# Seven block products in place of eight for q, k and v of a transformer block

## The chip, the cores and the metric

The kernel runs on one core of a Trainium2 chip. The metric is device time in microseconds for one execution; three runs took 2912.02, 2907.1 and 2908.67 us, so the median is 2908.67 us.

Five engines matter. TensorE (PE in the profile, with its weight loads as PEld) multiplies matrices into PSUM banks. VectorE (DVE) and ScalarE (ACT) read PSUM and write SBUF. GpSimd (POOL) works on SBUF. SyncE (SP) issues nearly all transfers. Each engine takes its instructions in order and waits on semaphores for the others.

## The reference

The input is 16 sequences of 224 tokens with 512 features, a condition vector per sequence, and a context of 750 tokens per sequence. All is float32. The part that changes is the first one, self-attention with 16 heads of 32 features:

```
shift_a, scale_a, gate_a, ... = split(silu(c) @ W_mod + b_mod, 6)
x_norm = layernorm(x) * (1 + scale_a) + shift_a
q, k, v = split(x_norm @ W_qkv + b_qkv, 3)
attn   = softmax(q k^T / sqrt(32)) v
x      = x + gate_a * (attn @ W_proj + b_proj)
```

Behind it come cross-attention to the context and an MLP (512 to 2048 to 512, GELU), each with its norm and residual.

## The kernel before

**Stages.** The kernel has three stages: self-attention (0 to about 728 us), cross-attention and the MLP. The output of each goes through DRAM (`x_self`, `x_cross`) to the next. Only self-attention is touched here.

**Order.** All engines' instructions are kept in the order in which the program gives them (class `Ordered`, lines 19 to 34): whatever is written earlier for an engine runs earlier on it. So the order of the Python calls is the order of each queue. A wrapper records every operation, and therefore nearly all of them carry line 28 in the profile; they are told apart by the names of their tiles.

**Self-attention.** The 16 sequences are taken two at a time (`PB` = 2), as 8 pairs. Two sequences together are 448 columns (`PN`). For a pair, `norm_begin`, `Norm.stats` and `Norm.apply` make the layer norm (statistics on VectorE, the rest on GpSimd, from tile `x` to tile `xn`); `turn_x` transposes a quarter of the features of both sequences on TensorE, and `modulate` writes the four results as four tiles `xt` of 128 x 448. `project_qk(p, m)` (line 445) makes one 128-row block of q or k for both sequences: four matmuls of 128x128 weights on 448 columns into one bank, and one eviction (q on VectorE, times the softmax scale; k on ScalarE). `project_v(p, c)` (line 462) makes v for one chunk of 112 tokens: four matmuls on 512 columns. A pair needs eight of the first and four of the second.

A pair's attention runs in 8 units, four groups `g` of four heads times two sequences `j` (the loop at line 627). A unit issues, in this order:

- `self_scores`: scores of the unit into `sc` (four PSUM banks, one buffer); VectorE reduces them to row maxima and splits these into three bf16 parts `nm`
- `finish`: VectorE normalizes the output of an earlier unit (a reciprocal and a product)
- slot 0 of the plan
- `self_weights` of the unit before: the scores again, transposed, less the maxima, into `sc`, and Exp on ScalarE into `pt`
- `max_rows`: the maxima transposed on TensorE into an "mm" bank, copied by VectorE
- `add_keys`: VectorE adds the two halves of `pt` into `acc`
- slot 1 of the plan
- `self_values`: values and the sums of the weights (from `acc`) into bank `o`

```
            if was:
                pt = self_weights(*was, row)
            row = max_rows(sa, ps_mm, nm)
            if was:
                acc = add_keys(pt)
            run(plan, (p, u, 1))
            if was:
                finish = self_values(*was, pt, acc)
```

**The plan** (`at_slot`, from line 503) fills the slots with work of other kinds: the rest of this pair's q and k, the output projection of the pair before (`project`, which also adds the residual to `x` and stores it), and the norm, transposes, v and first q and k of the next pair. Per pair, units 0, 2 and 4 hold two q or k products, unit 4 also the transposes, units 1 and 3 the output projection, units 5 and 6 v, unit 7 the next pair's first q and k. In the last pair the remaining parts are spread in halves, three to a unit. In the first pair, products for the modulation (`part`) take the place of the output projection.

**Buffers.** PSUM has eight banks: four for `sc`, three that go round under the name `mm` (projections, transposes, maxima), one for `o`. A bank is taken by the next tile once the last reader of its old tile is done. Input tiles `x` have six buffers and stay in SBUF until the residual is added.

The MLP stage already multiplies by seven block products (`combine`, `combine_right`, class `First`).

Of the kernel before, what the change touches and what calls it, by code (L numbers as in the profile page):

```python
# [8 lines left out]
F32 = mybir.dt.float32  # L9
# [28 lines left out]
def kernel(  # L38
# [187 lines left out]

    self_pools = ExitStack()
# [17 lines left out]
    for b in range(PB):  # L245
        xs[b] = load_x(sa, tokens(x, b), 6)
# [63 lines left out]
    def transpose_pair(pool, psum, xn, p, i_shift, i_scale, k):  # L310

        ps = psum.tile([P, 512], F32, name="mm")
        for t in range(PT):
            turn(ps[:, t * TP : (t + 1) * TP], xn[t // TC][:, t % TC, k * P : (k + 1) * P], ident[:TP, :TP])
        xt = pool.tile([P, PN], F32, name="xt", bufs=2 * KC)
        for j in range(PB):
            modulate(ps[:, j * N : (j + 1) * N], xt[:, j * N : (j + 1) * N], PB * p + j, k, i_shift, i_scale)
        return xt

# [10 lines left out]
    def weights_t(pool, psum, row, q_ap, k_ap, chunks, rows, bufs):  # L333

        st = psum.tile([P, HG, 512], F32, name="sc")
        n = len(chunks)
        for s in range(HG):
            mm(
                st[:rows, s, : n * N].rearrange("p (k t) -> p k t", k=n),
                ones16[s * HD : s * HD + NT, :rows],  # L340
                row[s * HD : s * HD + NT, :].unsqueeze(1).to_broadcast([NT, n, N]),
                start=True, stop=False,
            )
        for j, kc in enumerate(chunks):
            for s in range(HG):
                mm(
                    st[:rows, s, j * N : (j + 1) * N], k_ap(s, kc), q_ap(s),
                    start=False, stop=(j == n - 1),
                )
        pt = pool.tile([rows, HG, n * N], F32, name="pt", bufs=bufs)  # L350
        nc.scalar.activation(pt, st[:rows, :, : n * N], AF.Exp)
        return pt
# [83 lines left out]
    if True:  # L436
# [8 lines left out]
        def project_qk(p, m):  # L445
            ps = ps_mm.tile([P, 512], F32, name="mm")
            for k in range(KC):
                mm(
                    ps[:, :PN], (wq, wk)[m // KC][:, k, (m % KC) * P : (m % KC + 1) * P], xts[p][k],
                    start=(k == 0), stop=(k == KC - 1),  # L450
                )
                if k == 1:
                    yield
            t = sa.tile([P, PN], F32, name="qk", bufs=6)
            bm = bcol[:, o_qkv + m : o_qkv + m + 1]
            if m < KC:
                nc.vector.tensor_scalar(t, ps[:, :PN], bm, SCALE, ALU.add, ALU.mult)
            else:
                nc.scalar.activation(t, ps[:, :PN], AF.Identity, bias=bm)
            qk[p, m] = t  # L460

        def project_v(p, c):
            ps = ps_mm.tile([P, 512], F32, name="mm")
            for k in range(KC):
                mm(
                    ps[:TP, :H], xts[p][k][:, c * TP : (c + 1) * TP], wv[:, k, :],
                    start=(k == 0), stop=(k == KC - 1),
                )
            t = sa.tile([TP, H], F32, name="v", bufs=2 * PT)
            nc.scalar.copy(t, ps[:TP, :H])  # L470
            vs[p, c] = t

        def fetch(p):
            for b in range(PB * p, PB * (p + 1)):
                xs[b] = load_x(sa, tokens(x, b), 6)

        def norm_begin(p):
            for b in range(PB * p, PB * (p + 1)):
                xns[b] = sa.tile([TP, TC, H], F32, name="xn", bufs=PB)
                norms[b] = Norm(  # L480
                    [xns[b][:, c, :] for c in range(TC)], [xs[b][:, c, :] for c in range(TC)], TP
                )

        def turn_x(p, k):
            xts.setdefault(p, []).append(
                transpose_pair(
                    sa, ps_mm, [xns[PB * p + j] for j in range(PB)], p, i_shift_a, i_scale_a, k
                )
            )

        def project(p, t):
            b, c = PB * p + t // TC, t % TC
            if c == 0:
                gate[b] = gate_rows(sa, 0, b * N, TP, 2)
            ps = ps_mm.tile([P, 512], F32, name="mm")
            yield from project_heads(ps, at[p], wproj, t * TP)
            add_to_x(sa, ps[:TP, :H], xs[b][:, c, :], bproj, gate[b])
            if c == TC - 1:
                nc.sync.dma_start(out=x_self[b], in_=xs[b])
# [6 lines left out]

        for p in range(NP):
            if p < NP - 1:
                for g in range(1, KC):
                    at_slot(p, 2 * g - 2, 0, lambda p=p, g=g: whole(project_qk(p, g)))  # L510
                    at_slot(p, 2 * g - 2, 1, lambda p=p, g=g: whole(project_qk(p, KC + g)))
                for t in range(PT if p else 0):
                    at_slot(p, 1 + t // 2 * 2, t % 2, lambda p=p, t=t: whole(project(p - 1, t)))
            else:

                left = [(project_qk, p, m) for m in (1, KC + 1, 2, KC + 2)]
                left += [(project, p - 1, t) for t in range(2)]
                left += [(project_qk, p, m) for m in (3, KC + 3)]
                left += [(project, p - 1, t) for t in range(2, PT)]
                parts = [h for f, *args in left for h in halves(lambda f=f, args=args: f(*args))]  # L520
                for i, h in enumerate(parts):
                    at_slot(p, i // 3, i % 3 // 2, h)
# [18 lines left out]
            if n < NP:  # L541
                if n > 1:
                    at_slot(p, 0, 0, lambda n=n: fetch(n))
                at_slot(p, 1, 0, lambda n=n: norm_begin(n))
                for t in range(PT):
                    at_slot(
                        p, 1 + t // 2, t % 2, lambda n=n, t=t: norms[PB * n + t // TC].stats(t % TC)
                    )
                for j in range(PB):
                    at_slot(p, 1 + j, 1, lambda n=n, j=j: norms[PB * n + j].apply())  # L550
                for k in range(KC):
                    at_slot(p, 4, k // 2, lambda n=n, k=k: turn_x(n, k))
                for t in range(PT):
                    at_slot(p, 5 + t // 2, t % 2, lambda n=n, t=t: project_v(n, t))
                at_slot(p, 7, 0, lambda n=n: whole(project_qk(n, 0)))
                at_slot(p, 7, 1, lambda n=n: whole(project_qk(n, KC)))
# [35 lines left out]
        def self_values(p, g, j, pt, acc):  # L592
# [6 lines left out]
            if g == 0 and j == 0:  # L599
                at[p] = []  # L600
            if j == 0:
                at[p].append(sa.tile([P, PN], F32, name="at", bufs=2 * KC))
            return lambda: normalize(sa, o, at[p][g][:, j * N : (j + 1) * N])

        norm_begin(0)
# [8 lines left out]
        fetch(1)  # L614
# [3 lines left out]
        whole(project_qk(0, 0))  # L618
        whole(project_qk(0, KC))
        for t in range(PT):  # L620
            project_v(0, t)
        bproj = value_bias(sa, ps_mm, wproj, b_proj, o_qkv + 2 * KC, "bproj")

        units = [(p, g, j) for p in range(NP) for g in range(KC) for j in range(PB)]
        was = None
        finish = None
        for i, (p, g, j) in enumerate(units):
            u = g * PB + j
# [7 lines left out]
            row = max_rows(sa, ps_mm, nm)  # L636
            if was:
                acc = add_keys(pt)
            run(plan, (p, u, 1))
# [4 lines left out]
            left = len(units) - i  # L644
            if left == 16:
# [5 lines left out]
            if left in (10, 8):  # L651
                cnorms[0, left == 8].all()
            if left in (7, 6):
                Norm([first[7 - left][:TP]], [first[7 - left][:TP]], TP).all()
# [3 lines left out]
        for t in range(PT):  # L658
            whole(project(NP - 1, t))
        assert not plan  # L660
# [28 lines left out]

    def every(steps):  # L690
        for _ in steps:
            pass

    def combine(engine, a11, a12, a21, a22, s1, s2, s3, s4):

        yield engine.tensor_tensor(s1, a21, a22, ALU.add)
        yield engine.tensor_tensor(s3, a11, a21, ALU.subtract)
        yield engine.tensor_tensor(s2, s1, a11, ALU.subtract)
        yield engine.tensor_tensor(s4, a12, s2, ALU.subtract)

    def combine_right(engine, b11, b12, b21, b22, t1, t2, t3, t4):

        yield engine.tensor_tensor(t1, b12, b11, ALU.subtract)
        yield engine.tensor_tensor(t3, b22, b12, ALU.subtract)
        yield engine.tensor_tensor(t2, b22, t1, ALU.subtract)
        yield engine.tensor_tensor(t4, b21, t2, ALU.subtract)
# [636 lines left out]
```

## Time and profile before

| | us |
|---|---|
| median of three runs | 2908.67 (2907.1 to 2912.02) |
| span of the profiled execution, first to last instruction | 2906.1 |
| start, up to the first scores | 43.47 |
| first pair (83.55), then six pairs of 84.54 each | to 634.25 |
| last pair, up to the scores of its last unit | 63.07 |
| from there to the first work of cross-attention | 30.66 |

No time is listed for the profiled execution apart from its span; the span is 1.0 us below the fastest run and 2.6 us below the median.

Over the whole span the busy shares are PE 98%, PEld 62%, DVE 66%, POOL 41%, ACT 39%. A busy PE in these numbers holds matmuls whose ends are modelled, so the starts of the next instructions say more than the lengths. In a timeline line the first number is the start in us from the span's start, the second the length of the group, then engine, line, operation, output and input tiles, shapes, and the count; brackets give the idle time before it and what ended it.

### The profile page before, as it was taken

To read this page: it belongs to the slowest core of one execution; us is meant where nothing else is said; L and a number is where in the kernel's file an instruction comes from. 1 tells how busy PE (TensorE), PEld (TensorE's weight loads), DVE (VectorE), ACT (ScalarE), POOL (GpSimd) and SP (SyncE) were. 2 spreads that over 40 slices of the span, in tenths; PEclk is the share of its full clock that TensorE was granted. 3 is DMA by queue.
4 is the path that set the end of the run, shared out by engine and by line. 5 is a ranking of instruction groups with operands and counts; after the bars stand their busy time and mean duration, and the time that the engine had idled before them with its cause. 6 is when DMAs were issued, how large, how long until landed. Compare 5 with 4: busy or idle time off the path is not lost. (4 is left out here: it accounts for less than half of the span.)

```text
span 2906.1 us, 47040 instructions
## 1 busy us (share of the span) xinstructions
PE 2834.6 (98%) x19733; PEld 1810.3 (62%) x19733; DVE 1926.2 (66%) x2764; ACT 1119.7 (39%) x1402; POOL 1201.5 (41%) x1357
## 2 busy tenths in 40 slices
PE   8999999998999999999999999999979999999999
PEld 3444444444555565555656556556546888888888
DVE  4666776676478778787787787877775643444343
ACT  1222222221356655665566556655643112112211
POOL 1022222122356666676666766666551210221021
PEclk9999999998999999999999999999999999999999
DMA  5111110100100010100101100000013111110110
GB/s 191 59 33 33 32 33 10 60 11 24 57 32 24 23 35 24 35 26 21 35 24 35 35 19 28 27 33 24 22 44 107 55 37 37 44 58 29 45 44 30
DMA packets 55384, 114.43 MB, mean 39 GB/s; under 512 B 4308, under 2 KB 4372, under 8 KB 55172
## 3 DMA queue, kind: packets, MB, share of 16 engines
q1 hardware_dynamic: 54560, 110.58, 11.8%
q8 instruction: 155, 2.54, 0.4%
q10 hardware_dynamic: 612, 0.85, 0.1%
q14 instruction: 57, 0.47, 0.1%
HBM read 89.33 MB, written 22.09 MB: 38 GB/s over the span
## 5 line engine op out<-in xcount | busy, mean ns | idle before, releaser
L28 POOL TENSOR_TENSOR acc<-acc,pt 125x448 f32<-125x448 f32 x504 | 573.6, 1138 | 39.5
L28 ACT COPY pt<-sc 125x1792 f32<-125x1792 f32 x192 | 317.3, 1653 | 563.1 <-DVE top L28 510.1
L28 DVE TENSOR_TENSOR pt<-pt,o 125x896 f32<-125x896 f32 x384 | 394.2, 1081 | 88.1 <-PE o L28 85.5
L28 DVE TENSOR_TENSOR top<-top,sc 125x896 f32<-125x896 f32 x320 | 346.4, 1083 | 35.4 <-PE sc L28 28.7
L28 PE MATMUL mm<-wkvc,cxt 128*125 128x512 f32 x768 | 354.4, 604 | 6.9 <-ACT kt L28 6.9
L28 PE MATMUL mm<-cxt,wkvc 128*128 128x375 f32 x1024 | 355.0, 489 | 2.3 <-ACT cxt L28 2.3
L28 ACT ACTIVATE pt<-pt 125x896 f32<-125x896 f32 x384 | 338.4, 951 | 20.0 <-DVE pt L28 19.4
L28 POOL TENSOR_TENSOR upd<-upd,gate 112x512 f32<-112x512 f32 (+1 forms) x60 | 79.2, 1321 | 632.9 <-DVE upd L28 628.4
L28 POOL TENSOR_TENSOR acc<-pt 125x448 f32<-125x448 f32 x126 | 143.8, 1141 | 447.7 <-ACT pt L28 447.7
L28 PEld LDWEIGHTS mm<-cxt,wkvc 128*128 128x128 f32 x1024 | 185.6, 191 | 119.8 <-issue 16.6
L28 DVE RECIPROCAL at<-o 128x224 f32<-128x224 f32 x128 | 198.6, 1552 | 72.9 <-PE o L28 72.9
L28 PEld LDWEIGHTS mm<-wkvc,cxt 128*125 128x125 f32 x768 | 136.5, 187 | 171.5 <-issue 153.2
L28 ACT ACTIVATE pt<-sc 112x1792 f32<-112x1792 f32 x64 | 106.5, 1663 | 333.8 <-PE sc L28 333.8
L28 POOL TENSOR_TENSOR rstd<-mv,eps 112x2 f32<-112x2 f32 (+3 forms) x93 | 18.0, 193 | 508.8 <-DVE mv L28 508.8
L28 PE MATMUL sc<-qt,kt 32*125 32x224 f32 x3072 | 201.6, 377 | 14.0 <-ACT pt L28 13.4
L28 PE MATMUL mm<-xt,wqkv 128*128 128x448 f32 x512 | 208.6, 550 | 5.7 <-DVE xt L28 4.7
L28 DVE TENSOR_REDUCE m<-sc 112x8 f32<-112x1792 f32 x64 | 129.6, 2025 | 121.8 <-PE sc L28 121.8
L28 PEld LDWEIGHTS sc<-qt,kt 32*125 32x125 f32 x3072 | 133.1, 183 | 94.1 <-issue 33.8
L28 PE MATMUL o<-pt,vt 125*32 125x224 f32 x3072 | 158.6, 354 | 0.0
L28 PEld LDWEIGHTS mm<-xt,wqkv 128*128 128x128 f32 x512 | 92.0, 190 | 87.6 <-issue 80.4
L28 DVE TENSOR_REDUCE mc<-mm 112x8 f32<-112x512 f32 (+1 forms) x128 | 79.8, 665 | 98.3 <-PE mm L28 98.3
L28 ACT COPY mx<-a 128x512 f32<-128x512 f32 x26 | 15.2, 586 | 327.0 <-POOL upd L28 307.9
(185 smaller groups left out, 4656.5 us busy)
## 6 DMA issues: line engine op xcount, KB each, us to landing
cx<-in_ctx_dram SPq DMA_DIRECT2D x96, 250.0 KB
x<-in_x_dram SPq DMA_DIRECT2D x16, 448.0 KB
x_self<-x SPq DMA_DIRECT2D x16, 448.0 KB
x<-x_self SPq DMA_DIRECT2D x16, 448.0 KB
x_cross<-x SPq DMA_DIRECT2D x16, 448.0 KB
mx<-x_cross SPq DMA_DIRECT2D x28, 256.0 KB
w<-in_L_xcond_W_mlp_dram SPq DMA_DIRECT2D x7, 1024.0 KB
xr<-x_cross SPq DMA_DIRECT2D x28, 256.0 KB
```

Of the source, the lines that this page charges most:

```text
L28: return lambda *args, **kw: self.tc.keep_in_program_order(f(*args, **kw))
```

## The change

**Seven products.** For a pair, x is seen as a matrix of two by two blocks: features 0 to 255 and 256 to 511, first and second sequence. Each of the three weight matrices is cut into two by two blocks of 256. With four sums of blocks of x (`data_blocks`) and four of each weight (`weight_blocks`), the four blocks of the result come from seven block products instead of eight (`seven`). `project_qk(p, i, r)` makes rows `r` and `r + 2` of q (`i` = 0) or k (`i` = 1) for both sequences: seven products of two matmuls on 224 columns. `project_v(p, c)` makes two token chunks of v, one of each sequence: seven products of two matmuls on 256 columns.

Products are numbered by the block pair that they multiply, and run in the order 1, 2, 6, 5, 7, 3, 4. Three banks are used: a holds 1, then 6, 7 and 4 on top; c holds 2; b holds 5, then 3 on top. After a product, ScalarE or VectorE copies the bank to its place in the result (`keep`), or VectorE adds the bank to what is there (`add`).

**The plan.** A third slot comes behind `add_keys`, and `add_keys` itself now stands behind slot 1. A seven is cut in four steps: products 1 and 2, and product 6, in slot 0; 5 and 7 in slot 1; 3 and 4 in slot 2. Units 0 and 1 hold rows 1 and 3 of q and of k, units 2 and 3 the output projection and the transposes of the next pair, units 4 and 5 v, units 6 and 7 rows 0 and 2 of the next pair's q and k. Groups of heads go in the order 0, 2, 1, 3. In the last pair the sevens take units 0 to 3 in halves and the output projection of the pair before units 4 to 7.

**Sums.** The block sums of x (four of 128 x 448) are made on GpSimd in unit 3; those of the weights (twelve of 128 x 512) on VectorE before the first unit.

**Norm and residual.** x is loaded straight into `xn` (two buffers), and the norm is made in place. For the residual, `fetch_rest` loads x again, one chunk of 112 tokens at a time into three buffers, a unit ahead of the output projection, and each chunk is stored on its own. The softmax scale moves from the eviction of q into the Exp.

The core of the diff:

```diff
+    def seven(product, bank, keep, add):
+        a = bank()
+        product(a, 1, True)
+        keep((0, 0), a)
+        c = bank()
+        product(c, 2, True)
+        add((0, 0), c)
+        yield
+        product(a, 6, False)
+        keep((0, 1), a)
+        yield
+        b = bank()
+        product(b, 5, True)
+        keep((1, 1), b)
+        product(a, 7, False)
+        add((1, 1), a)
+        yield
+        product(b, 3, False)
+        add((0, 1), b)
+        product(a, 4, False)
+        keep((1, 0), a)
...
+    def data_blocks(engine, tt, x0, x1):
+        every(combine_right(
+            engine, x0[:, lo2], x1[:, lo2], x0[:, hi2], x1[:, hi2],
+            tt[:, 0], tt[:, 1], x1[:, lo2], tt[:, 2],
+        ))
+        return {
+            1: x0[:, lo2], 2: x0[:, hi2], 3: x1[:, hi2], 4: tt[:, 2],
+            5: tt[:, 0], 6: tt[:, 1], 7: x1[:, lo2],
+        }
...
+        def project_qk(p, i, r):
...
+            def keep(at, ps):
+                m = o_qkv + i * KC + r + 2 * at[0]
+                if at == (1, 1):
+                    nc.vector.tensor_scalar(place(at), ps[:, :N], bcol[:, m : m + 1], None, ALU.add)
+                else:
+                    nc.scalar.activation(place(at), ps[:, :N], AF.Identity, bias=bcol[:, m : m + 1])
+            def add(at, ps):
+                nc.vector.tensor_tensor(place(at), ps[:, :N], place(at), ALU.add)
...
+        def fetch_rest(p, t):
+            b, c = PB * p + t // TC, t % TC
+            xr[b, c] = sa.tile([TP, H], F32, name="xr", bufs=3)
+            nc.sync.dma_start(out=xr[b, c], in_=tokens(x, b)[:, c, :])
...
+        def one(u):
+            return (u, 0), (u, 0), (u, 1), (u, 2)
+
         for p in range(NP):
             if p < NP - 1:
-                for g in range(1, KC):
-                    at_slot(p, 2 * g - 2, 0, lambda p=p, g=g: whole(project_qk(p, g)))
-                    at_slot(p, 2 * g - 2, 1, lambda p=p, g=g: whole(project_qk(p, KC + g)))
+                for i in range(2):
+                    steps(p, one(i), lambda p=p, i=i: project_qk(p, i, 1))
                 for t in range(PT if p else 0):
-                    at_slot(p, 1 + t // 2 * 2, t % 2, lambda p=p, t=t: whole(project(p - 1, t)))
+                    at_slot(p, 1 + t // 2, t % 2, lambda p=p, t=t: fetch_rest(p - 1, t))
+                    at_slot(p, 2 + t // 2, t % 2, lambda p=p, t=t: whole(project(p - 1, t)))
...
                 for k in range(KC):
-                    at_slot(p, 4, k // 2, lambda n=n, k=k: turn_x(n, k))
-                for t in range(PT):
-                    at_slot(p, 5 + t // 2, t % 2, lambda n=n, t=t: project_v(n, t))
-                at_slot(p, 7, 0, lambda n=n: whole(project_qk(n, 0)))
-                at_slot(p, 7, 1, lambda n=n: whole(project_qk(n, KC)))
+                    at_slot(p, 2 + k // 2, 1, lambda n=n, k=k: turn_x(n, k))
+                at_slot(p, 3, 1, lambda n=n: x_sums(nc.gpsimd, n))
+                if n + 1 < NP:
+                    at_slot(p, 4, 0, lambda n=n: fetch(n + 1))
+                for c in range(TC):
+                    steps(p, one(4 + c), lambda n=n, c=c: project_v(n, c))
+                for i in range(2):
+                    steps(p, one(6 + i), lambda n=n, i=i: project_qk(n, i, 0))
...
             row = max_rows(sa, ps_mm, nm)
+            run(plan, (p, u, 1))
             if was:
                 acc = add_keys(pt)
-            run(plan, (p, u, 1))
+            run(plan, (p, u, 2))
             if was:
                 finish = self_values(*was, pt, acc)
```

## The prediction

> **What bounds the kernel now.** I read the windows first (which engine fills which stretch), then the engines' timelines of the fourth pair of sequences, and last the places where TensorE waited.
>
> One pair in the steady state, by the windows (columns: length; busy us and instructions of PE, PEld, DVE, ACT, POOL; clock, DMA share, GB/s):
>
> ```profile
> 127.02:211.56 84.54, 83.45 (x645) 41.47 (x641) 59.18 (x96) 18.18 (x16) 17.44 (x20) 1.00 0.10 28
> ...
> 697.00:698.00 1.00, 1.00 (x16) 0.66 (x12) 0.00 (x0) 0.00 (x0) 0.89 (x1) 0.76 0.00 0
> 698.00:699.00 1.00, 1.00 (x12) 0.58 (x7) 0.00 (x0) 0.00 (x0) 0.00 (x0) 0.50 0.35 102
> ```
>
> PE works 83.45 of 84.54 us: each us of its work counts, and each us in which it waits counts as much. DVE is at 70%. One unit of that stage on PE, by the timeline (start, length):
>
> ```profile
> 316.51 1.03 PE L28 MATMUL sc<-qk 32*112 32x224 f32 x16
> 317.47 3.27 PE L28 MATMUL mm<-xt,wqkv 128*128 128x448 f32 x8
> 320.67 0.40 PE L28 MATMUL sc<-mrow,ones 3*112 3x448 bf16 x4
> 320.91 0.93 PE L28 MATMUL sc<-qk 32*112 32x224 f32 x16
> 321.77 0.27 PE L28 MATMUL mm<-ident,nm 112*128 112x112 bf16 x2
> 321.88 3.23 PE L28 MATMUL mm<-xt,wqkv 128*128 128x448 f32 x8
> 325.04 0.96 PE L28 MATMUL o<-pt,v 112*32 112x224 f32 x16
> 325.82 0.56 PE L28 MATMUL o<-acc,ones 112*32 112x224 f32 x8
> ...
> 764.48 1.68 PE L28 MATMUL mm<-xt,wqc 128*128 128x224 f32 x8
> 765.99 1.45 PE L28 MATMUL mm<-ident,cx 125*128 125x125 f32 x12
> ```
>
> No gap, and the next unit's scores start at 326.31: scores 0.96, a block of projections in slot 0, weights 1.10, maxima 0.11, a block in slot 1, values 0.78, sums 0.49. VectorE in the same unit, and in the one unit type where PE does wait:
>
> ```profile
> 317.61 2.02 DVE L28 TENSOR_REDUCE m<-sc 112x8 f32<-112x1792 f32 x1 [0.68 <-PE sc L28]
> ...
> 320.42 1.54 DVE L28 RECIPROCAL at<-o 128x224 f32<-128x224 f32 x1
> 321.99 0.39 DVE L28 TENSOR_TENSOR at<-o,at 128x224 f32<-128x224 f32 x1
> 322.30 0.67 DVE L28 TENSOR_SCALAR qk<-mm,bcol 128x448 f32<-128x448 f32 x1
> ...
> 323.87 1.08 DVE L28 TENSOR_TENSOR acc<-pt 112x896 f32<-112x896 f32 x1
> ...
> 343.44 0.26 PE L28 MATMUL mm<-ident,nm 112*128 112x112 bf16 x2 [0.42 <-DVE qk L28]
> 344.37 3.25 PE L28 MATMUL mm<-xt,wqkv 128*128 128x448 f32 x8 [0.67 <-DVE xt L28]
> ```
>
> See that an eviction of slot 0 stands behind reduction, split and reciprocal: PE left the scores at 317.47 and had done the q product by 320.67, but DVE took it at 322.30, 4.83 after the scores. Today that rarely hurts, as the three "mm" banks go round; in unit 4, where two transposed banks are added, PE waited on just that eviction (0.42) and on the transposes' (0.67).
>
> **The change, part by part.** All times "at" are from the moment PE leaves a unit's scores.
>
> *PE work.* A float matmul is two passes here. Per pair, q and k have 64 passes of 448 columns, 0.376 apart (a block of 8 takes 3.16 to 3.20: 8 x 0.376 = 3.01, and 0.15 to 0.19 at the change from small to full tiles). They become 4 x 7 x 2 x 2 = 112 passes of 224. The row at 764.48 is this shape: 8 in 1.51, 0.189 each. So 24.1 becomes 21.2. v has 32 passes of 512 columns at 0.429 (350.54 to 354.16 for 8) and gets 56 of 256; the MLP's passes of that shape start 1.73 per 8, 0.216 each: 13.7 becomes 12.1. Saved 4.5 a pair, 36 in eight.
>
> *Wait 1: the bank of the fifth product.* A "seven" takes three banks (a, c, b) while the maxima's transposes take one too, and there are three. Slot 0 uses a and c, the maxima the third, so slot 1's b gets c's bank, free once DVE has added c. That add stands behind the reciprocal: it starts at 4.83 and takes 0.39, so P5 starts at 5.25. PE gets there: q or k unit 12 passes (2.46) + 1.10 + 0.11 = 3.67, waits 1.58; v unit 2.78 + 1.21 = 3.99, waits 1.3. Then 16 passes (3.17, or 3.6 for v) with the evictions of P5 and P7 in time (DVE 6.2 to 6.6 and 6.9 to 7.3; P3 and P4 want them at 6.8 and 7.5), values, sums and scores 2.23: 10.63 for q/k units, 11.1 for v units. In units 0 and 1 two bn_stats pairs (0.82 each) also precede the key sums, which end at 9.2 instead of 8.3; PE wants them at 9.2: 10.7. Queued behind PE's wait are P7, P3, P4, values and the next scores, so the whole unit moves.
>
> *Wait 2: the key sums.* add_keys moves behind slot 1 on DVE. In units 2 and 3 slot 1 now holds an output projection and two transposes. PE: 3.61 + 1.10 + 0.11 + 3.57 + 0.86 = 9.25, values until 10.03. DVE must first do upd (8.57), then four xt modulations (1.67, the row at 343.31; until 10.85), then the sums (11.93). PE waits 1.98: 13.46 instead of 11.48.
>
> A pair: 2 x 10.7 + 2 x 13.46 + 2 x 11.1 + 2 x 10.63 = 91.8, of which 12.9 is waiting; before 84.54 (9.80, 10.62, 9.80, 10.62, 12.66, 10.62, 10.62, 9.80). +7.2 each in pairs 1 to 6: **+43**.
>
> *Start.* PE has 22.7 of products (two sevens of q and k, two of v) instead of 19.8 before the first unit. DVE makes 12 weight sums (the MLP's 128x512 rows: 0.68) and POOL four sums of xt (1.14, by acc<-acc,pt 125x448), and P6 wants the third of each: xt is ready at 21.7, POOL's third at 24.1, so q ends at 28.0; wk's third sum at 29.6, k ends at 33.4; wv's at 35.2, v ends at 45.6 instead of 39.9. **+5.7** (ends: 2.9 if all sums hide, 15.7 if all 12.8 us of them show).
>
> *First pair.* No output projection fills units 2 and 3: DVE's chain sets 10.0 and 14.1; unit 1 holds a seven and two modulation parts, 16.2; with 7.4, 2 x 11.1 and 2 x 10.63 it is 91.2 against 83.55: **+7.7**.
>
> *Last pair.* Only two sevens are left, in halves: units of 8.0 and 9.1 in turn, then 8.72 with half projections; in each, reduction to key sums to next scores sets it. Seven units 60.4 instead of 63.07. The last unit keeps filler, so its tail is 13.2 instead of 16.45 (697.32 to 713.77, at half clock): **-5.9**.
>
> *Clock.* The windows show clock 0.76, then 0.50, after PE waits of 1.59 and 0.45 (694 to 697). A wait of 1.62 at 736.10 was followed by none. 1.98 lies between. A fall lasts 3.4 us at least (796.5 to 799.9), 1.7 us of work. Twelve such waits in pairs 1 to 6: 0 to 20; I take half, **+10**. [...]
>
> *Costed at nothing.* Scale inside Exp: the same 1.66 us instruction. Norm in place: the same instructions; x is fetched from unit 4 on, 42 us ahead of its statistics. Residual chunks: 0.9 MB more per pair at 28 GB/s; on SP, chunk 3's load stands behind the store of chunk 1, which waits for POOL, and it is needed a unit (13 us) later; were it late, POOL's sums of xt would follow it and P6 of unit 4 with them. ACT: 18 short copies instead of 8 long, +3 us on 18. DVE: 18 adds of 0.39 to 0.42 and six copies of 0.43 less four evictions of 0.68, +7 on 59, harmless but for its place. POOL's sums of xt stand behind two residual adds and end their third at 2.4 of unit 4, where P6 is wanted at 1.9: the wait for P5 covers that.
>
> Sum: 43 + 5.7 + 7.7 - 5.9 + 10 = +61. The profiled span is 2906.1; the median run is 2.6 longer, and that I add: **2969**.
>
> **The rivals.**
> - *The waits are hidden* (other side): DVE comes to c's add before PE wants b. It decides below 4.4 us of waiting a pair (7.5 of start and ends + 6 x (w - 5.7) = 0) against my 12.9. With none: 6 x -5.7 + 5.7 - 4 - 5.9 = -38, 2870. For it: DVE has 30% free. Against: its order shows in every unit, and three banks are three.
> - *Only wait 1 is missing* (b gets a free bank): w = 4.0, no gain, 2906. *Only wait 2 is missing*: 2935.
> - *The 1.58 waits lower the clock too*: 24 more chances, 1.7 each, all taken: +41, 3010. They are shorter than the 1.62 that did nothing, but by a hair.
> - *Short passes don't pay*: weight loads take 0.19 for 128 columns; at 0.216 per pass +3.0 a pair, 2993. The row at 764.48 says 0.189.
>
> **How the numbers follow.** Mine 0.64 (own range 2945 to 2995); waits hidden 0.06; wait 1 missing 0.05; wait 2 missing 0.08; clock 0.13; slow passes 0.04. Range 2930 to 3015 takes in all but the first two rivals and some overshoot. Faster by over 0.2% (a run tells no less): 0.08; within: 0.03; slower: 0.89.
>
> **What would show it.** Right: pairs of about 92 us; PE idle of 1.3 to 1.6 ahead of each fifth product, released by DVE; in units 2 and 3 some 2 us ahead of o<-acc, released by DVE acc; products 0.19 and 0.216 per pass; DVE's xt modulations ahead of acc; clock falls after units 2 and 3; first scores near 49. Wrong: PE over 97% busy within a pair, or its waits on ACT, POOL or DMA.

## The result, and the profile after

The changed kernel takes 3022.38 us (median of four runs, 3021.26 to 3022.95); the kernel before, on the same chip, 2910.35 us (2907.1 to 2913.03). The ratio is 1.0387, with a 95% interval of 1.0372 to 1.0401: 112 us slower. The forecast was 2969, within 2930 to 3015: the direction was right, and the loss was almost twice the one foretold.

The page's line of busy times and the window of the fourth pair (columns as in the prediction; the same pair took 84.53 before, with PE busy for 83.44 of it):

```profile
PE 2854.6 (94%) x20309; PEld 1930.1 (64%) x20309; DVE 1992.3 (66%) x2936; ACT 1141.1 (38%) x1482; POOL 1247.6 (41%) x1389
...
343.39:442.34 98.95, 86.62 (x717) 56.46 (x713) 66.19 (x116) 20.91 (x26) 22.79 (x24) 0.93 0.12 33
```

The pair has 12.3 us in which PE waits, where there was 1.1. And although less arithmetic is asked of PE, its busy time has gone up by 3.2: the clock in this window is 0.93, where it was 1.00.

**A q or k unit.** PE's timeline in unit 6 of that pair:

```profile
421.76 1.78 PE L28 MATMUL mm<-xt,wqkv 128*128 128x224 f32 x8
423.38 0.97 PE L28 MATMUL mm<-xtt,wb 128*128 128x224 f32 x4
424.28 0.40 PE L28 MATMUL sc<-mrow,ones 3*112 3x448 bf16 x4
424.51 0.93 PE L28 MATMUL sc<-qk 32*112 32x224 f32 x16
425.37 0.27 PE L28 MATMUL mm<-ident,nm 112*128 112x112 bf16 x2
427.02 1.02 PE L28 MATMUL mm<-xtt,wb 128*128 128x224 f32 x4 [1.38 <-DVE qk L28]
427.88 0.92 PE L28 MATMUL mm<-xt,wqkv 128*128 128x224 f32 x4
428.64 0.97 PE L28 MATMUL mm<-xt,wb 128*128 128x224 f32 x4
429.45 0.92 PE L28 MATMUL mm<-xtt,wqkv 128*128 128x224 f32 x4
430.30 0.96 PE L28 MATMUL o<-pt,v 112*32 112x224 f32 x16
```

and VectorE's over the same stretch:

```profile
421.90 2.03 DVE L28 TENSOR_REDUCE m<-sc 112x8 f32<-112x1792 f32 x1 [2.23 <-PE sc L28]
...
424.70 1.55 DVE L28 RECIPROCAL at<-o 128x224 f32<-128x224 f32 x1
426.28 0.39 DVE L28 TENSOR_TENSOR at<-o,at 128x224 f32<-128x224 f32 x1
426.59 0.38 DVE L28 TENSOR_TENSOR qk<-mm,qk 128x224 f32<-128x224 f32 x1
```

The fifth product starts 5.26 after PE left the scores. It waits for the addition of c's bank at 426.59, and that addition was ready to run at about 423.5, when the second product was done, but stood in VectorE's queue behind the reduction, the split and the reciprocal.

**Unit 2** of the next pair. PE at its end and at the start of unit 3, then VectorE and GpSimd at the same time:

```profile
474.03 0.96 PE L28 MATMUL o<-pt,v 112*32 112x224 f32 x16
477.82 0.97 PE L28 MATMUL o<-acc,ones 112*32 112x224 f32 x8 [2.83 <-DVE acc L28]
478.73 1.85 PE L28 MATMUL sc<-qk 32*112 32x224 f32 x16
480.51 5.64 PE L28 MATMUL mm<-wproj,at 128*112 128x512 f32 x8
```

```profile
474.05 1.76 DVE L28 TENSOR_SCALAR xt<-mm,mod_t 128x224 f32<-128x224 f32 x4
475.72 2.04 DVE L28 TENSOR_TENSOR acc<-pt 112x896 f32<-112x896 f32 x1
...
475.56 1.26 POOL L28 TENSOR_TENSOR xr<-xr,upd 112x512 f32<-112x512 f32 x1
```

The key sums (`acc`) begin 0.16 after GpSimd began the residual addition, and take 2.04 instead of 1.08. PE waits 2.83, and the next scores take 1.85 instead of 1.02 and the next projection 5.64 instead of 3.69. Three windows from there (the column with two decimals behind POOL is the clock):

```profile
477.40:480.80 3.40, 2.98 (x25) 1.61 (x26) 0.52 (x2) 0.00 (x0) 0.00 (x0) 0.54 0.59 202
480.80:484.20 3.40, 3.40 (x5) 1.23 (x5) 3.26 (x6) 0.00 (x0) 0.00 (x0) 0.50 0.02 5
484.20:487.60 3.40, 3.40 (x28) 1.63 (x27) 2.00 (x4) 0.29 (x1) 0.58 (x1) 0.96 0.00 0
```

From the end of the wait on PE runs at half clock for 6.8 us. The same happens behind unit 3. In the records of the whole stage up to cross-attention it runs at half clock for 99 us, against 17 before.

**Two places outside the pairs.** At the start, VectorE makes the weight sums while GpSimd sums x, and PE waits for the third of them:

```profile
22.95 0.67 DVE L28 TENSOR_TENSOR wb<-wqkv 128x512 f32<-128x512 f32 x1
23.66 1.50 DVE L28 TENSOR_TENSOR wqkv<-wqkv 128x512 f32<-128x512 f32 x1
25.08 1.61 DVE L28 TENSOR_TENSOR wb<-wb,wqkv 128x512 f32<-128x512 f32 x1
...
26.84 3.10 PE L28 MATMUL mm<-xtt,wb 128*128 128x224 f32 x8 [3.51 <-DVE wb L28]
```

And at the start of cross-attention, SyncE, ScalarE and PE:

```profile
837.76 2.86 SPq L28 DMA_DIRECT2D x_self<-xr  x2
...
840.08 1.53 ACT L28 COPY cxt<-mm 128x500 f32<-128x500 f32 x3 [23.11 <-DMA x_self<-xr]
...
841.67 5.06 PE L28 MATMUL mm<-cxt,wkvc 128*128 128x375 f32 x8 [5.81 <-ACT cxt L28]
```

ScalarE may not write the transposed context before the last residual chunks have been stored, since it lies at the addresses of `xr`. PE waits 5.81, and then runs at half clock.

**Where the 114.8 us between the two profiled spans (2906.1 and 3020.9) lie:**

| stretch | before | after | difference | forecast |
|---|---|---|---|---|
| start, to the first scores | 43.47 | 54.30 | +10.8 | +5.7 |
| first pair | 83.55 | 93.78 | +10.2 | +7.7 |
| pairs 1 to 6 | 507.23 | 593.81 | +86.6 | +43, and +10 for the clock |
| last pair and its tail | 93.73 | 92.30 | -1.4 | -5.9 |
| first cross operation to first cross scores | 14.32 | 20.84 | +6.5 | 0 |
| the rest | 2163.78 | 2165.84 | +2.1 | 0 |

A pair in the middle is 98.95, 14.4 longer. Its units, 0 to 7: 10.79, 10.79, 14.82, 17.57, 12.29, 11.16, 10.76, 10.77. The start is the least certain row: the kernels below that leave it as it is in the change have their first scores between 52.61 and 55.39.

### The profile page after: what moved, and what is told of

Read it like the earlier page. It is cut to its first block, busy times and chain, and to the rows that moved or that the text cites. A ratio compares the mean times of both kernels' runs of the same rounds, so it can differ in the third digit from the quotient of the medians.

```text
span 3020.9 us, 48655 instructions
## 1 busy us (share of the span) xinstructions
PE 2854.6 (94%) x20309; PEld 1930.1 (64%) x20309; DVE 1992.3 (66%) x2936; ACT 1141.1 (38%) x1482; POOL 1247.6 (41%) x1389
## 5 line engine op out<-in xcount | busy, mean ns | idle before, releaser
L28 POOL TENSOR_TENSOR rstd<-mv,eps 112x2 f32<-112x2 f32 (+3 forms) x93 | 27.7, 298 | 832.4 <-DVE mv L28 832.4
L28 PEld LDWEIGHTS sc<-qt,kt 32*125 32x125 f32 x3072 | 133.7, 184 | 94.8 <-issue 33.8
L28 PE MATMUL sc<-qk 32*112 32x224 f32 x2048 | 136.1, 383 | 0.0
L28 ACT ACTIVATE qk<-mm,bcol 128x224 f32<-128x224 f32 x96 | 42.9, 447 | 230.8 <-PE mm L28 230.8
```

The lines of the kernel that those rows point to most:

```text
L28: return lambda *args, **kw: self.tc.keep_in_program_order(f(*args, **kw))
```

## The experiments

The theory after this reading: three orders in the queues (the normalization ahead of c's addition, slot 1's work ahead of the key sums, GpSimd's residual addition beside the key sums) make PE wait, the longest of these waits lower the clock, and nothing else is wrong with the seven products. The rivals: the gaps cost little and it is the clock; or the engines around PE have too little room, so that a wait taken away returns elsewhere.

### Key sums ahead of slot 1 again

```diff
+            if was:
+                acc = add_keys(pt)
             run(plan, (p, u, 1))
-            if was:
-                acc = add_keys(pt)
             run(plan, (p, u, 2))
```

> One edit: the key sums (add_keys) go back in front of slot 1, as in the kernel before; all else stays changed. Theory K (the key sums, queued behind the transposes' evictions in units 2 and 3, and the clock falls that their wait sets off, are most of the loss): units 2 and 3 go from 14.8 and 17.6 us to about 11.5 each, unit 4 from 12.3 to 11.2, no half clock within pairs 1 to 6, a pair from 99.0 to about 88.4; the time falls by some 65 us to about 2956 us. Rival B (the waits for the bank of the fifth product are the larger part and set off the clock falls): the clock still falls in each pair, a pair stays above 95 us and the time above 2995 us.

Measured: 2980.96 us, ratio 1.0247 (1.0232 to 1.0262). A pair takes 92.58 (94.8 in the two of six in which the clock still fell, in unit 4): units 11.54, 11.54, 11.39, 11.39, 13.61, 11.33, 10.9, 10.9. Units 2 and 3 lost their wait and their half clock. But two new waits stand in PE's timeline of that pair:

```profile
341.91 1.02 PE L28 MATMUL mm<-xt,wb 128*128 128x224 f32 x4 [0.56 <-DVE qk L28]
...
384.18 1.12 PE L28 MATMUL mm<-wb,xtt 128*112 128x256 f32 x4 [2.02 <-POOL xtt L28]
```

In units 0 and 1 the third product now stands behind the key sums: VectorE copies the fifth product out of b only after them. In unit 4 the sixth product comes sooner than GpSimd's third sum of x. So the key sums' place was worth 41 us, less than expected, since part of what it frees is waited for elsewhere.

### Normalization ahead of the scores

```diff
-            self_scores(p, g, j, nm)
             if finish:
                 finish()
+            self_scores(p, g, j, nm)
             run(plan, (p, u, 0))
```

> One edit: the normalization of the earlier unit (reciprocal and product) is written in front of the scores instead of behind them, so that c's add no longer stands behind the reciprocal; key sums stay behind slot 1. Theory B (the fifth product waits for c's bank, and c's add waits for the reciprocal): the 1.38 us ahead of the fifth product goes to nothing and about 0.75 us appears ahead of the weights (0.4 in v units), as the reduction starts 1 us later; q and k units go from 10.77 to about 10.1, a pair from 99.0 to about 95, the time to about 2996 us. If the fifth product waits for something else, its wait stays and the time stays near 3022 us.

Measured: 2976.9 us, ratio 1.0233 (1.0216 to 1.025), 19 us better than expected. The wait for c's bank is gone in all units; units 0 and 1 take 9.84, 6 and 7 9.82, and a pair 90.2 to 94.0. In its place PE waits for the split maxima, which moved back by the reciprocal, and the wait for the key sums is where it was:

```profile
328.45 0.40 PE L28 MATMUL sc<-mrow,ones 3*112 3x448 bf16 x4 [0.56 <-DVE m L28]
...
357.93 0.59 PE L28 MATMUL o<-acc,ones 112*32 112x224 f32 x8 [2.83 <-DVE acc L28]
```

The reciprocal's place on VectorE was the cause of the first wait. The clock fell behind 10 of the 12 waits of 2.83 in pairs 1 to 6, mostly for 3.4 us: half-clock time before cross-attention went from 99 to 58 us. Of the surplus, some 8 us lie in units 2 to 4 of the six pairs, where the clock was at half for a shorter time, and some 7 in the q and k units, which gained 0.95 each and not 0.67.

### The same gaps, filled with transposes

Eighteen transposes of the identity, whose results nobody reads, are written between the values and the sums in units 2 and 3: TensorE works through most of the wait, but the wait's end stays where it is.

```diff
+            if fill:
+                ps = mm_bank()
+                for _ in range(fill):
+                    turn(ps[:, :P], ident, ident)
             sums(o, [acc], TP)
...
-                finish = self_values(*was, pt, acc)
+                finish = self_values(*was, pt, acc, 18 if u in (2, 3) and p < NP - 1 else 0)
```

> One addition, and no result uses it: in units 2 and 3 of pairs 0 to 6 TensorE makes 18 transposes of the identity between values and key sums, about 2.2 us, where it would wait 2.8. Theory K's second half (the idle stretch halves the clock, and the halved clock costs some 5 us a pair beyond the wait): no half clock within pairs 1 to 6, a pair goes from 99.0 to about 94, the time to about 2988 us. Rival (the clock falls are only a sign, their cost is hidden behind VectorE): the clock stays full and the time stays within 5 us of 3022.

Measured: 3007.73 us, ratio 1.0335 (1.032 to 1.0351). At the end of unit 3 of pair 4, PE's timeline has:

```profile
483.91 2.18 PE L28 MATMUL mm<-ident 128*128 128x128 f32 x18
486.83 0.59 PE L28 MATMUL o<-acc,ones 112*32 112x224 f32 x8 [0.73 <-DVE acc L28]
```

Pairs 1, 2 and 4 take 94.9 to 95.0 with no half clock, pairs 3 and 5 96.6 with one fall of 3.4 us each in unit 4. So the fallen clock was worth 4.0 us of the 98.95, and the waits themselves the larger part: the rival that it is all the clock is out. The total is 20 us above what was expected: the expectation took some 5 us in each of seven pairs, 34 in all. The six pairs gained 19.8 together, and what stands around them got longer (first scores at 55.39, first pair 94.95, last pair 66.22 against 63.51).

### No residual on GpSimd

This kernel leaves out the product with the gate and the addition of the residual: what is stored is x without them.

```diff
-            add_to_x(sa, ps[:TP, :H], res, bproj, gate[b])
+            upd = sa.tile([TP, H], F32, name="upd", bufs=2)
+            nc.vector.tensor_tensor(upd, ps[:TP, :H], bproj, ALU.add)
```

> Leaves out the gate product and the residual add of self-attention on GpSimd (x is stored as it came); VectorE's instructions stay. Theory C (the key sum took 2.04 us instead of 1.08 because GpSimd's residual work reads SBUF at the same time): the key sum of unit 2 takes 1.08 us and the wait there falls from 2.83 to about 1.9; in unit 3 GpSimd's sums of xt may still run beside it, and there it stays near 2. By the waits alone a pair loses 1 to 2 us and the time 6 to 13; if the shorter wait also spares the clock after unit 2, up to 3 us a pair more, 2990. If the key sum stays at 2.04 in unit 2, theory C is wrong.

Measured: 2982.68 us, ratio 1.0251 (1.0236 to 1.0266). VectorE, GpSimd, PE, and the window of a pair:

```profile
458.15 1.08 DVE L28 TENSOR_TENSOR acc<-pt 112x896 f32<-112x896 f32 x1
...
458.38 1.84 POOL L28 TENSOR_TENSOR xtt<-xt 128x448 f32<-128x448 f32 x1 [9.37 <-DVE xt L28]
...
459.29 0.59 PE L28 MATMUL o<-acc,ones 112*32 112x224 f32 x8 [1.79 <-DVE acc L28]
...
424.83:517.06 92.23, 80.81 (x716) 53.69 (x712) 64.00 (x116) 20.92 (x26) 13.29 (x16) 1.00 0.13 36
```

With GpSimd's residual work out of the way the same instruction on VectorE takes 1.08, PE waits 1.79, the clock stays at 1.00 in this pair (it fell behind 2 of the 12 such waits in pairs 1 to 6), and the units are 10.79, 10.79, 13.4, 13.39, 11.16, 11.16, 10.77, 10.77. So 0.96 us on one VectorE instruction, twice a pair, with the clock falls that it sets off, makes most of the way from 92.2 to 98.95. The expectation had the key sum stay near 2 in unit 3, beside GpSimd's sums of x; it takes 1.08 there too. A sum of x runs beside it in units 2 and 3 here, but starts 0.23 after it (458.38 and 471.77), and it is this sum that takes 1.84 and 1.85, where 1.13 is its time alone: of the two, the one that starts second takes longer here.

### Early sums of wq

```diff
+        left[0] = weight_blocks(nc.vector, ws, wq, "wb0")
         rows = [part_rows(i) for i in range(2)]
         make_columns()
...
-            left[i] = weight_blocks(nc.vector, ws, w, f"wb{i}")
+            if i:
+                left[i] = weight_blocks(nc.vector, ws, w, f"wb{i}")
```

> The changed kernel, but the four sums of wq's blocks are written ahead of the bias columns, so that VectorE makes them at about 16.8 us (wq has landed by then at 385 GB/s) and not beside GpSimd's sums of x. Theory: of the 10.8 us that the start got longer, some 3 come from the weight sums that take 1.50 to 1.61 instead of 0.68 beside GpSimd, and from the half clock behind the wait of 3.51; the four sums then take 0.68 each, GpSimd's take 1.1 each, q's P6 starts near 26 instead of 26.84 (it now waits for GpSimd's third sum), and q's passes run at full clock: first scores 1 to 3 us sooner, 3019 to 3021 in all. Rival, the start is only longer by the work: the sums make the bias columns 1.5 us later and with them everything behind: first scores at 54.3 to 56, 3022 to 3024. The pairs stay at 94 to 102 in both.

Measured: 3020.43 us, ratio 1.0381 (1.0365 to 1.0397): no difference to the change that these runs can tell. The sums are made from 16.44 on, the second to fourth at 0.68 to 0.69 each, and q's sixth product then waits for GpSimd:

```profile
27.02 1.78 PE L28 MATMUL mm<-xtt,wb 128*128 128x224 f32 x8 [1.71 <-POOL xtt L28]
```

The first scores are 1.4 sooner (52.88), which is within the range of the unchanged start (52.61 to 55.39), and the first pair is 0.9 longer. The product is not sooner than 26.84, since the modulation of x is later by what the sums took: the rival saw this right. The clock still falls once, for 3.4 us from 20.70 on, behind a new wait of 1.71 ahead of the transposes; what is gained is that the sixth product's group runs at full clock (1.78 instead of 3.10).

### A pool of its own for the residual chunks

```diff
+    xr_pool = self_pools.enter_context(tc.tile_pool(name="xr", bufs=3))
     sa = self_pools.enter_context(tc.tile_pool(name="sa", bufs=3))
...
-            xr[b, c] = sa.tile([TP, H], F32, name="xr", bufs=3)
+            xr[b, c] = xr_pool.tile([TP, H], F32, name="xr", bufs=3)
```

> The changed kernel, but the residual chunks have a pool of their own, placed ahead of the pool of the other self-attention tiles, so that other addresses are reused by the transposed context of the cross-attention. Theory: the 6.5 us by which the start of the cross-attention got longer come from the stores of the last residual chunks, which have to read these addresses first, and from the half clock behind that wait: from the first cross operation to the first cross scores 14 to 16 us instead of 20.84 (before: 14.32), 3014 to 3018 in all. Rival, any tile of the self-attention's pool holds the context up as long (the last attention's operands are read as late): 20 to 21, 3021 to 3024.

Measured: 3015.46 us, ratio 1.0365 (1.0351 to 1.038). From the first cross operation to the first cross scores it takes 13.90 (20.84 in the change, 14.32 before):

```profile
836.96 2.79 PE L28 MATMUL mm<-cxt,wkvc 128*128 128x375 f32 x8 [0.67 <-ACT cxt L28]
```

The 6.5 us were the reuse of the chunks' addresses and the half clock behind that wait, and no work at all.

### Three orders mended

```diff
+            late = p < NP - 1 and u not in (2, 3)
+            if was and not late:
+                acc = add_keys(pt)
             run(plan, (p, u, 1))
-            if was:
+            if was and late:
                 acc = add_keys(pt)
...
             self_scores(p, g, j, nm)
-            if finish:
-                finish()
             run(plan, (p, u, 0))
+            if finish:
+                finish()
...
-        yield engine.tensor_tensor(t3, b22, b12, ALU.subtract)
         yield engine.tensor_tensor(t2, b22, t1, ALU.subtract)
+        yield engine.tensor_tensor(t3, b22, b12, ALU.subtract)
```

The sums of the weights (`combine`) change places in the same way: the one for the sixth product comes second. Both functions serve the MLP too, whose stretch stays as it was (behind the first cross scores 2165.40, in the change 2165.84).

> The changed kernel with three edits in the order of the self-attention: the key sums are written ahead of slot 1 in units 2 and 3 and in the whole last pair (elsewhere behind it, as in the change), the normalization of the values is written behind slot 0 and not ahead of it, and of the block sums the one that P6 takes is made second and not third. Theory: all the waits of TensorE in a pair have these three causes (the normalization ahead of c's sum, slot 1's work ahead of the key sums, GpSimd's third sum ahead of unit 4's P6), and the falls of the clock come from them: units 0 and 1 9.84, units 2 and 3 11.4, unit 4 10.2 to 11.1, unit 5 10.2, units 6 and 7 9.82, a pair 82.5 to 83.5 (before 84.54), no half clock in pairs 1 to 6; start and cross-attention as in the change: 2912 to 2930 in all. Rival, VectorE and GpSimd together have too little room, and each wait that is taken away comes back at another tile: pairs of 88 to 92, 2950 to 2985.

Measured: 2923.48 us, ratio 1.005 (1.0036 to 1.0064). The window of a pair, and what PE still waits for in it:

```profile
308.30:393.80 85.50, 80.90 (x717) 53.85 (x713) 66.59 (x116) 20.91 (x26) 22.84 (x24) 1.00 0.14 39
```

```profile
315.86 1.02 PE L28 MATMUL mm<-xt,wb 128*128 128x224 f32 x4 [1.14 <-DVE qk L28]
...
356.04 1.12 PE L28 MATMUL mm<-wb,xtt 128*112 128x256 f32 x4 [0.94 <-POOL xtt L28]
```

Nothing but the order of instructions on VectorE and GpSimd was changed, and 99 of the 112 us are back. Pairs 1 to 6 show no half clock at all. The pair is 85.5 and not 83, because small waits are left: in units 0 and 1 the copy of the fifth product out of b now stands behind the reciprocal (1.14), in unit 4 GpSimd's second sum of x is still late (0.94, with 0.24 and 0.42 behind it), and units 6 and 7 wait 0.34. That is the rival's mechanism, with 2 to 3 us a pair where the rival had 5 to 9.

### All of it together

The three orders, the early sums of wq and the pool for the chunks; the edits are those above.

> The three edits in the order of the self-attention, and with them the early sums of wq and the residual chunks' own pool. Theory: what the three runs beside it gain adds up: pairs of 82.5 to 83.5, first scores at 51 to 54, cross-attention's start 14 to 16 us: 2900 to 2920 in all, so about the kernel before (2909); it is faster than that only if the pairs save more (1 to 2 us each in six) than the start costs. Rival, the waits come back elsewhere: 2940 to 2980.

Measured: 2916.04 us, ratio 1.0024 (1.0014 to 1.0033). Cross-attention starts in 14.04 instead of the 20.41 of the run above, which is most of the difference; the pairs are the same 85.5. The first scores come 0.95 sooner and the first pair is 1.6 longer, so the next kernel leaves the early sums out. The longer first pair can hardly be theirs, though: it takes 86.06 here and 85.90 in the next kernel without them. In both the clock is at half for 6.8 us behind a wait of 1.96, in the run above for 3.4 us behind the same wait.

### Two orders more

```diff
+            ahead = p < NP - 1 and u < 2
+            if finish and ahead:
+                finish()
             self_scores(p, g, j, nm)
             run(plan, (p, u, 0))
-            if finish:
+            if finish and not ahead:
                 finish()
...
-                    at_slot(p, 2 + t // 2, t % 2, lambda p=p, t=t: whole(project(p - 1, t)))
+                    if t < PT - 1:
+                        at_slot(p, 2 + t // 2, t % 2, lambda p=p, t=t: whole(project(p - 1, t)))
...
                 at_slot(p, 3, 1, lambda n=n: x_sums(nc.gpsimd, n))
+                if 0 < p < NP - 1:
+                    at_slot(p, 3, 1, lambda p=p: whole(project(p - 1, PT - 1)))
```

> The three edits in the order of the self-attention and the residual chunks' own pool (without the early sums of wq), and two edits more: the normalization is written ahead of the scores in units 0 and 1 (behind slot 0 in the others), and in unit 3 the fourth output projection is written behind the transposes and GpSimd's sums of x. Theory: what waiting is left in a pair of the run with the three edits (1.14 in units 0 and 1 for VectorE's sum behind the key sums and the normalization, 0.95 in unit 4 for GpSimd's sums and some 1.3 behind it) goes: units 0 and 1 9.84, units 2 and 3 11.4, unit 4 10.0 to 10.8, a pair 82 to 83 instead of 85.5; with the first scores at 53, the last pair at 57.5 and the cross-attention's start at 14: 2890 to 2902 in all, 0.2 to 0.6% below the kernel before. Rival, the waits only move: the transposes' evictions now stand ahead of the fourth projection's bank, unit 3 grows by what unit 4 loses, pairs of 84.5 to 85.5: 2906 to 2916.

Measured: 2906.83 us (2903.99 to 2910.17) against 2910.2 (2906.98 to 2912.69), ratio 0.9989 (0.998 to 0.9998). The window of a pair, and the wait that was moved into unit 3:

```profile
305.97:389.91 83.94, 80.62 (x716) 53.82 (x713) 65.56 (x116) 20.93 (x26) 22.78 (x24) 1.00 0.14 39
```

```profile
344.61 3.69 PE L28 MATMUL mm<-wproj,at 128*112 128x512 f32 x8 [0.85 <-DVE mrow L28]
```

Units 0 and 1 take 9.84 as expected. Unit 4 gave 1.2, of which unit 3 took 1.07 back, since the fourth projection now finds its bank still held (0.85). So both theories were partly right, and the seven products, with their waits mostly gone, end a tenth of a per cent below the eight, just clear of noise. Little of that comes from the pairs. In the two profiles, whose spans are level (2906.5 and 2906.1), the start costs 8.6 more (first scores at 52.11) and the first pair 2.4; the six pairs save 2.2 together (0.6 in the one shown, 0.4 in the mean); and the last pair with its tail saves 8.3, where the kernel before ran at half clock for 17.1 us and this one for 6.8.

## Why the prediction was wrong in size

By its own steps:

- **PE work**: the pass was right, the saving too large. The timelines show 0.19 per pass of 224 columns (four start 0.76 before the next, 427.88 to 428.64) and 0.22 of 256 (0.86 for four, 48.09 to 48.95). But the two groups behind the first take 0.81 and 0.85, and in the pair without the residual, from start to start and less the waits, the 112 passes of q and k take 23.2 (0.207 each, 0.189 foretold) and the 56 of v 12.8; counted in the same way, it was 25.3 and 14.4 before. So 3.7 a pair is saved on them and not 4.5. PE's busy time fell from 83.4 to 80.8, by only 2.6: the maxima's transposes, whose end the next product used to cover, now stand ahead of a wait and count 0.27 and not 0.11, and the values in units 2 and 3 likewise. The forecast's pair hides this, since a wait that ends when VectorE is done is shorter for a PE that comes later: its 78.9 of work and 12.9 of waiting came out as 80.8 and 11.4. The rival of slow short passes had 0.216: within a group it is out, but the mean of 0.207 is two thirds of the way to it.
- **Wait 1, c's bank**: right in cause and place. The product starts at 5.26, 5.25 was foretold; PE came to it at 3.88 and not 3.67, so it waits 1.38, not 1.58. Units with v wait 1.15 (foretold 1.3). The order tests show that the reciprocal ahead of the addition is the cause: written elsewhere, the wait goes.
- **Wait 2, key sums**: this is the step that failed. Its sum was "DVE must first do upd (8.57), then four xt modulations (1.67 ...), then the sums (11.93)", with the key sums at the 1.08 of a quiet unit (by these numbers the wait was 1.90; 1.98 was put down). But the two residual operations on GpSimd follow `upd` at once, so in just these units the sums run beside them: 2.04, a wait of 2.83 and not 1.98. With 1.08 put back by taking GpSimd's work away, units 2 and 3 are 13.4 (foretold 13.46) and the pair 92.23 (foretold 91.8). The trace of before had the row that says so, in a unit with an output projection, VectorE's sums and then GpSimd's addition beside them:

```profile
313.40 1.24 DVE L28 TENSOR_TENSOR acc<-pt 112x896 f32<-112x896 f32 x1
...
313.77 2.00 POOL L28 TENSOR_TENSOR x<-x,upd 112x512 f32<-112x512 f32 x1
...
317.54 1.27 POOL L28 TENSOR_TENSOR x<-x,upd 112x512 f32<-112x512 f32 x1
```

  There VectorE came first and GpSimd's 1.27 became 2.00. Here GpSimd comes first, and VectorE's 1.08 becomes 2.04: `xr` runs from 475.56 to 476.82, and `acc` is done 0.94 after that, at 477.76.
- **Clock**: mis-sized, as a consequence. "Half" of twelve falls of 1.7 us of work was taken, +10. At 1.98 that was too much rather than too little (below: 4 of 18 waits of 1.79 and 2.02 were followed by a fall); but waits of 2.76 to 2.84 lowered the clock in 12 of 12 cases, for 6.8 us in ten of them. By the filled gaps it is 4.0 a pair, some 24 in six.
- A pair, then: 91.8 foretold; 92.2 with the key sums at 1.08; 94.9 with them at 2.04 (with the gaps filled, at full clock); 98.95 with the clock. Of the 2.7 between 92.2 and 94.9, 2.1 are the two waits and 0.6 lies in unit 4, where a cast on VectorE takes 0.82 beside GpSimd's sums of x and not 0.18. With the clock term the forecast had 93.5 a pair; the 5.5 more are 33 of the missing 54. The other 21 are in the next steps.
- **Start**: +10.8 and not +5.7. The wait of 3.51 for the third weight sum has the same cause (VectorE takes 1.50 and 1.61 beside GpSimd's sums of x, and 0.68 to 0.69 for three of the early sums) and has 3.4 us of half clock of its own behind it, from 27.08 on; xt was ready 1.3 later too (23.02 and not 21.69), since the second part of `w_mod` landed later (PE takes it at 14.13, and at 12.80 before). The same start gave first scores at 52.61 to 55.39 in other runs, so part of the 5.1 that was missing may be chance; how the rest splits is open.
- **First pair**: +10.2 (foretold +7.7). Half of the difference is unit 3, 15.36 for 14.1; the clock is at half from 81.70 to 91.94, into this unit, behind a wait of 1.96. This was not tested by itself. **Last pair**: -1.4 (foretold -5.9). Units of 12.31 and 9.37 stand there where 9.1 was foretold, and 3.4 us of half clock come with the first of them. With the key sums ahead of slot 1 in the last pair and the other orders, its seven units are 57.5, less than the 60.4 foretold, so it is these orders and not the work.
- **Costed at nothing**: the residual chunks were weighed by their loads, not by the addresses that they hold at the end of the stage: +6.5. The last 2.1, behind the first cross scores, are within what the other kernels have there, 2163.4 to 2167.0. GpSimd's sums of x were free in the change, but it was the half clock of unit 4 that covered them: at full clock they cost the 0.6 above, and with the key sums ahead of slot 1 they showed at once (2.02 in unit 4).
- **The rivals**: PE's waits, 12.3 a pair, come to the 12.9 of the forecast, so neither wait was missing. No wait of 1.38 in pairs 1 to 6 lowered the clock, so the rival that put 24 more falls there is out; only the last of them, in unit 7 of pair 6, is 1.89 long and did. The range ended at 3015 since each fall was taken as 3.4 us long, and no case had an instruction on VectorE itself become longer.

## What to carry to other kernels

When an operation is moved on one queue, its duration has to be looked up beside what the other engine does at the new place: for VectorE's key sums that was GpSimd's timeline (1.08 alone, 2.04 behind GpSimd's addition). A wait on TensorE is paid twice if it lowers the clock, as the two of 2.83 in a pair did here, for 4.0 us more, so a range for a change that adds such waits has to reach to all of them falling. And a change that saves TensorE work in small blocks is worth only what the order of the evictions leaves of it: here five edits of order, and one of addresses, turned +112 us into -3. The saving itself has to be taken from whole units, with the changes between the blocks in it: 4.5 us a pair by the pass were 3.7 from start to start, and 2.6 in busy time.

## What the runs showed of the hardware

- Instructions of VectorE and GpSimd took longer beside each other: `acc` 1.08 alone, 2.04 behind GpSimd's residual addition, and 1.08 again with that addition left out; weight sums 0.68 alone, 1.50 to 1.61 beside GpSimd's sums of x; GpSimd's addition 1.27 alone, 2.00 behind VectorE's key sums, and its sum of x 1.13 alone, 1.84 behind them.
- The granted clock fell to a half behind waits of 2.76 to 2.84 in the change (12 of 12), and in its pairs 1 to 6 it stayed there for 3.4 or 6.8 us. Of the waits of 2.83 in the run with the normalization ahead, 10 of 12 were followed by a fall; of those of 2.02 with the key sums ahead of slot 1, 2 of 6; of those of 1.79 without the residual on GpSimd, 2 of 12; and in the change none of those of 1.38.
- Why equal waits did and didn't lower it, no run tested. The clock records of the kernel before and of the change give this much: their 31 half-clock stretches begin and end at whole multiples of one length from each other, to 0.01 (but for the end of the last one in each, which the end of the run cuts): 27.08 to 3017.16 in the change is 876 times 3.4133 us. With the time from the first scores to cross-attention (43.47 to 727.98 before, 54.30 to 834.19 in the change) cut into pieces of that length, a piece at full clock was followed by half clock 17 times, and PE was idle for 1.63 to 2.76 us of it; it was followed by full clock 377 times, and PE was idle for at most 1.70.
